# The third batch's second layer by eighths, and its expert mixing paired with the fourth's

## The chip, the cores and the metric

The kernel runs on one core of a Trainium2 chip, all of it in 32-bit floats. The metric is the device time of one execution in microseconds (us); the kernel before took 3224.32 us, the median of three runs (3222.8 to 3226.45).

The core has five instruction streams that run side by side and wait for each other through semaphores: TensorE (PE; its weight loads are shown as PEld) multiplies matrices, VectorE (DVE), ScalarE (ACT) and GpSimd (POOL) work on tiles, and SyncE (SP) issues nearly all of this kernel's DMAs, in program order. An instruction of SP that has to wait holds up every later DMA of that queue.

## The reference

Four batches of 2048 rows with 512 columns pass a windowed attention and then a feed-forward layer whose weights differ from batch to batch: a small gate, averaged over the batch, gives eight numbers, and the weights are the base weights plus eight expert weights scaled by them.

```python
# attention: 16 heads of 32, windows of 128 rows that see themselves and both neighbours, residual, layer norm
# then, for a batch with rows x1 (2048 x 512):
g  = mean over rows of (relu(x1 @ gw1.T + gb1) @ gw2.T + gb2)       # 8 numbers
W1b = W1 + sum_e g[e] * TW1[e]      # 2048 x 512      b1b likewise
W2b = W2 + sum_e g[e] * TW2[e]      # 512 x 2048      b2b likewise
out = x1 + layernorm(gelu(x1 @ W1b.T + b1b) @ W2b.T + b2b)
```

One mixed weight is 4 MB, and the experts of a layer are 32 MB, so each batch reads 64 MB of experts if it reads them for itself.

## The kernel before

**Attention first, then the feed-forward part.** The first 1674.4 us are attention, the gate and the layer norms. The rest is the feed-forward part in 16 blocks of 512 rows, `K` = 0 to 15; batch `b` is K // 4 and `k` = K % 4 the block in it. PE has its matmuls back to back; DVE, ACT, POOL and SP work beside it.

**The first layer of a block** is four *sets* (`c` = 0, 2, 4, 6), each a Winograd scheme of seven products in place of eight. A product is four matmuls 128x128x256 (L1023). `begin` (L1042) issues products A11 and S1 of a set; `middle` (L1065) issues A12, S2, S4, S3 and, after S2, calls `end` (L1086) of the set *before*, which issues that one's last product A22. Two sums on DVE lie in a set: `cpb` (L1080) after S4 and `cpv` (L1083) after S3; A22 adds into the bank of S3, so it can't start before `cpv` was read from there. Four places `step()` in `middle` let the mixing on DVE go on: before S2, before `cpb`, between `cpb` and `cpv`, and after `cpv`. The last set of a block (c = 6) has its `end` called by the second layer, after that one's first few matmuls.

**The second layer** has two forms. `second` (L1157) is seven products of 16 matmuls 128x256 (L1143; 112 in all), `end` of the last set coming after two of them. `second_deep` (L1237), used where the batch is in `DEEP`, applies the scheme twice, seven by seven products ("by eighths"), each four matmuls 128x128x128 (L1308; 196 in all). Of its outer products `o` = 0 to 6 each needs four differences of activations on DVE (`inner_sums`, L1233), held in two tiles of the `exps` pool. They are made during the outer product before, but those of o = 0 only when the last activations of c = 6 exist, and `end` of that set comes after the first four matmuls. POOL computes `t1`, `t2` (L1105, L1106, L1111) after each set and, at o = 2, a further difference into `t1` (L1344), the right side of o = 6. The layer norm's statistics of half of the rows come at o = 6 before the sum that follows `inner(4)`. DEEP is the fourth batch alone.

**Mixing.** The generator `mixer` (L106) goes through 64 chunks in a fixed order (batch, layer, eight chunks of two row groups), each with eight experts: one load of 512 KB (L123, three ahead, four buffers `exps`), one scalar_tensor_tensor (STT) `acc += g[e] * expert` on DVE (L155), and after the eighth four sums (L163 to L166) and the stores of the Winograd factors to DRAM (m1d, m2d, or m3d for DEEP). One `next(blend)` is one STT or the four sums: 9 steps to a chunk, 576 in all. 226 are placed in attention (MIXED, L961), the rest in the blocks: `mixing(1, 1, 1, 1)` in a set (2, 1, 1, 1 at c = 2; 0, 1, 0, 1 in block 0 and a batch's last block), and `mixing(3, 2, 3, 2, 2, 3, 2)` over the products of `second`.

**Inner sums of the deep weights.** `inner_mixer` (L174) has 14 steps for a deep batch: two loads of 256 KB from m3d into an `exps` buffer (two steps ahead), four sums on DVE (L205 to L208), three stores. Eight steps run in the second layer of block 11, six in the sets of block 12.

**Loads of the second layer's weights.** `load_second` (L1120) fetches 512 KB (`w2s`, six buffers; 14 loads in a plain block, 28 in a deep one) each time that a group of second-layer matmuls has been issued, so the six first loads of a block go out in the second layer of the block before. In a batch's last block `more_sums` (L1094) also loads the next batch's first-layer factors (5.5 MB, `load_first`).

Of the kernel before, what the change touches and what calls it, by code (L numbers as in the profile page):

```python
# [9 lines left out]
F32 = mybir.dt.float32  # L10
# [24 lines left out]
def sandwich(ctx: ExitStack, tc: tile.TileContext, x, w_qkv, gw1, gb1, gw2, gb2, w1, b1, w2, b2, tw1, tb1, tw2, tb2, out):  # L35
# [23 lines left out]
    gw1_sb = const.tile([P, KC, D], F32, name="gw1_sb")  # L59
# [20 lines left out]
    DEEP = (NB - 1,)  # L80
# [25 lines left out]
    def mixer():  # L106

        todo = [(b, s, c, e) for b in range(NB) for s in range(2) for c in range(HC) for e in range(NX)]
        ets, accs = {}, {}
# [5 lines left out]
        def load(n):  # L115
            b, s, c, e = todo[n]
            base, exps = ((w1, tw1), (w2, tw2))[s]
            if e == 0:
                acc = mix.tile([P, 2, D], F32, tag="acc", name=f"acc_{b}_{s}_{c}")
                nc.sync.dma_start(acc, halves(base)[c])  # L120
                accs[b, s, c] = acc
            et = mix.tile([P, 2, D], F32, tag="exps", bufs=4, name=f"exps_{b}_{s}_{c}_{e}")
            nc.sync.dma_start(et, halves(exps[e])[c])  # L123
            ets[n] = et
# [20 lines left out]
        for n in range(3):  # L145
            load(n)
        yield
        for n, (b, s, c, e) in enumerate(todo):
            if n + 3 < len(todo):
                load(n + 3)  # L150
            for f in late:
                f()
            late = []
            acc = accs[b, s, c]
            nc.vector.scalar_tensor_tensor(acc, ets.pop(n), g_all[b][:, e : e + 1], acc, ALU.mult, ALU.add)  # L155
            yield
            if e == NX - 1:
                del accs[b, s, c]
# [10 lines left out]
        for f in late:  # L169
            f()  # L170

    issued = {b: 0 for b in DEEP}

    def inner_mixer(b):  # L174

        todo = [(o, h) for o in order_deep for h in range(2)]
        loaded, late = {}, []

        def load(n):
            o, h = todo[n]  # L180
            two = slice(2 * h, 2 * h + 2)
            et = mix.tile([P, 4, 2, P], F32, tag="exps", bufs=4, name=f"inner_{b}_{o}_{h}")
            nc.sync.dma_start(et[:, :2], m3_d[b][:, o, 0:8:7, two, :])
            nc.sync.dma_start(et[:, 2:], m3_d[b][:, o, 3:7:3, two, :])
            loaded[n] = et

        def store(n, et):
# [7 lines left out]
        for n in range(2):  # L195
            load(n)
        yield
        for n in range(len(todo)):
            for f in late:
                f()  # L200
# [1404 lines left out]
```

## Time and profile before

| what | value |
|---|---|
| median of the runs (3) | 3224.32 us |
| the profiled execution: its time, its span | 3224.83 us, 3223.0 us |
| attention, gate, norms: until | 1674.4 us |
| PE busy | 3197.1 us (99%) |
| DVE, ACT, POOL busy | 2278.8 (71%), 1576.5 (49%), 676.5 us (21%) |
| granted TensorE clock | 0.998 |
| moved by DMA | 688.88 MB |
| expert loads `exps<-in_tw` | 512 of 512 KB |
| STTs (L155) | 512, 697.1 us, 1362 ns each |

The span runs from the first instruction to the last; the profiled execution's time is 1.8 us longer, and lies 0.5 us above the median. Busy shares are of the span. In the views of stretches each row begins with a stretch (us from the start of the span) and its length, then the busy time and count of instructions on each engine, the granted clock (PEclk), the mean busy share of the DMA engines and the rate. In a timeline a row gives start, duration, engine, line, operation, tile written from tiles read, the shape, and in brackets for how long the engine had been idle and what ended it. A view of waits gives the engine and the tile and line that wait, what they wait for, the sum in us, the count and the longest. A group of instructions has "busy, mean ns of one | idle time before, and what ended it".

### The profile page before, as it was taken

What the parts mean: (1) busy time and instruction counts of PE and PEld (TensorE: products, weight loads), DVE (VectorE), ACT (ScalarE), POOL (GpSimd) and SP (SyncE); (2) the same over time, 40 slices, a digit from 0 to 9 for tenths busy, and PEclk for the clock granted to TensorE, in tenths of its full rate; (3) what the DMA queues carried; (4) which work ended last, traced back from release to release, by engine and by line L of the source; (5) the groups of instructions that cost most, each with busy time, mean ns of one, the idle gap of its engine ahead of it and who ended that gap; (6) DMA issues with size and microseconds to landing.
All of it is one profiled execution on the core that took longest, in us unless ns stands there. A gap on an engine that the chain in (4) does not pass through costs nothing.

```text
span 3223.0 us, 61653 instructions
## 1 busy us (share of the span) xinstructions
PE 3197.1 (99%) x23862; PEld 2697.0 (84%) x23862; DVE 2278.8 (71%) x3307; ACT 1576.5 (49%) x4332; POOL 676.5 (21%) x847
## 2 busy tenths in 40 slices
PE   9999999999999999999999999999999999999998
PEld 7788888888788888878768888888888888889998
DVE  5766666888998889888865665677657667554555
ACT  3777777777777777777761222112222112222222
POOL 0111111111111111110112322323322323332233
PEclk9999999999999999999999999999999999999999
DMA  2111112455555556554677889999899999874555
GB/s 87 54 57 54 40 60 80 138 189 163 193 193 168 178 177 200 194 174 151 211 277 277 310 309 345 355 337 330 311 330 361 341 326 322 305 246 155 193 187 170
DMA packets 363334, 688.88 MB, mean 214 GB/s; under 512 B 27161, under 2 KB 115353, under 8 KB 357026
## 3 DMA queue, kind: packets, MB, share of 16 engines
q1 hardware_dynamic: 363042, 684.94, 61.4%
q8 instruction: 189, 3.10, 0.4%
q14 instruction: 103, 0.84, 0.1%
HBM read 567.39 MB, written 117.44 MB: 212 GB/s over the span
## 4 chain that ended last, share of the span: by engine, by line
PE 94%; DVE 2%; DMA 2%; ACT 1%; POOL 0%; issue 0%; SPq 0%; POOLq 0%; DVEq 0%; ACTq 0%
PE pm L518 23%; PE px L1023 13%; PE ptp L686 11%; PE px L1143 7%; PE sc L649 7%; PE pz L1023 6%; PE po L707 5%; PE pz L1143 5%; PE py L1023 3%; PE py L1143 3%; PE px L1308 2%; PE py2b L1143 2%; PE pz L1308 1%; PE pm L582 1%; PE ptx L340 1%; PE pto L311 1%
## 5 line engine op out<-in xcount | busy, mean ns | idle before, releaser
L155 DVE SCALAR_TENSOR_TENSOR acc<-exps,g,acc 128x1024 f32<-128x1024 f32 x512 | 697.1, 1362 | 66.1 <-DMA exps<-in_tw 60.1
L658 DVE TENSOR_REDUCE nm<-sc 128x2 f32<-128x768 f32 (+1 forms) x512 | 449.2, 918 | 206.8 <-PE sc L649 201.8
L671 ACT ACTIVATE pr<-sc,nm 128x384 f32<-128x384 f32 (+1 forms) x1024 | 572.8, 592 | 11.3 <-DVE nm L658 11.1
L691 ACT COPY prT<-ptp 128x512 f32<-128x512 f32 x732 | 382.9, 595 | 281.3 <-PE ptp L686 281.1
L686 PEld LDWEIGHTS ptp<-ident,pr 128*128 128x128 f32 x2944 | 318.0, 141 | 102.3 <-issue 89.8
L686 PE MATMUL ptp<-ident,pr 128*128 128x128 f32 x2944 | 378.7, 278 | 0.0
L1060 ACT COPY py<-px 128x512 f32<-128x512 f32 x63 | 36.0, 571 | 662.6 <-PE px L1023 662.4
L1023 PE MATMUL px<-tT,w 128*128 128x256 f32 x1512 | 350.1, 379 | 0.6 <-DVE cpv L1083 0.6
L1023 PEld LDWEIGHTS px<-tT,w 128*128 128x128 f32 x1512 | 286.9, 190 | 40.0 <-DVE cpv L1083 1.0
L649 PE MATMUL sc<-k,q 32*128 32x384 f32 (+2 forms) x2816 | 243.2, 423 | 3.7 <-ACT pr L671 3.5
L671 ACT ACTIVATION_READ_ACCUMULATOR pr<-sc,nm 128x1 f32 x1024 | 236.5, 231 | 0.0
L1080 DVE TENSOR_TENSOR cpb<-pz,cpb 128x512 f32<-128x512 f32 x63 | 43.4, 689 | 268.8 <-PE pz L1023 240.1
L96 POOL TENSOR_SCALAR ve_b<-mv_b 128x1 f32<-128x1 f32 x64 | 42.8, 669 | 819.2 <-DVE mv_b L94 819.2
L707 PEld LDWEIGHTS po<-prT,v 128*32 128x32 f32 x5888 | 152.2, 110 | 50.9 <-ACT pr L671 25.4
L707 PE MATMUL po<-prT,v 128*32 128x128 f32 x5888 | 189.7, 275 | 0.2
L649 PEld LDWEIGHTS sc<-k,q 32*128 32x128 f32 x2816 | 118.7, 184 | 74.4 <-issue 53.9
L1143 PE MATMUL px<-w2s,u 128*128 128x256 f32 x784 | 175.1, 379 | 0.0
L518 PE MATMUL pm<-xnT,wqkv 128*128 128x256 f32 x720 | 172.2, 382 | 0.0
L1105 POOL TENSOR_TENSOR t<-u 128x512 f32<-128x512 f32 x60 | 79.9, 1332 | 434.8 <-ACT u L1035 434.8
L1143 PEld LDWEIGHTS px<-w2s,u 128*128 128x128 f32 x784 | 149.0, 190 | 20.2
L518 PEld LDWEIGHTS pm<-xnT,wqkv 128*128 128x128 f32 x720 | 132.0, 190 | 16.7
L1074 ACT COPY cpb<-px 128x512 f32<-128x512 f32 x63 | 36.9, 585 | 182.0 <-PE px L1023 182.0
(295 smaller groups left out, 5911.6 us busy)
## 6 DMA issues: line engine op xcount, KB each, us to landing
exps<-in_tw SPq DMA_DIRECT2D x512, 512.0 KB, 6.0
w2s<-m2d SPq DMA_DIRECT2D x168, 512.0 KB, 8.1
w2s<-m3d SPq DMA_DIRECT2D x84, 512.0 KB, 4.7
acc<-in_w SPq DMA_DIRECT2D x64, 512.0 KB, 6.1
x<-in_x SPq DMA_DIRECT2D x64, 256.0 KB, 4.2
m1d<-acc SPq DMA_DIRECT2D x64, 256.0 KB, 6.3
w<-m1d SPq DMA_DIRECT2D x16, 1024.0 KB, 7.9
fxT<-xTd SPq DMA_DIRECT2D x16, 1024.0 KB, 8.5
```

Source lines behind the costliest of these rows:

```text
L155: nc.vector.scalar_tensor_tensor(acc, ets.pop(n), g_all[b][:, e : e + 1], acc, ALU.mult, ALU.add)
L518: nc.tensor.matmul(bank[u not in chain][:, half, :], lhsT=a[:, kc, ts(half, P)], rhs=b[:, kc, :], start=(u not in (2, 3, 4) and half == kc ...
L649: nc.tensor.matmul(scs[r // 2][:, r % 2, col : col + nj * W], lhsT=q[rows, g, ts(W_ % WB, W)], rhs=k_of[kb][rows, g, j0 * W : (j0 + nj) * ...
L658: nc.vector.tensor_reduce(st["nm"][:, h : h + 2], scs[u][:, :, : nk * W], AX.X, ALU.max, negate=True)
L671: nc.scalar.activation(pr[:, : nk * W], scs[r // 2][:, r % 2, : nk * W], AF.Exp, bias=st["nm"][:, h : h + 1], accum_out=st["den"][:, h : h ...
L686: nc.tensor.transpose(pt[:, r, :], st["pr"][g * 4 + r][:, ts(j, W)], ident)
L691: nc.scalar.copy(prT, pt)
L707: nc.tensor.matmul(po[r * E : (r + 1) * E, n, :], lhsT=v_of[kb][:, jj, h * E : (h + 1) * E], rhs=prT[:, r, :], start=(j == 0), stop=(j == ...
L1023: nc.tensor.matmul(bank[:, f, :], lhsT=factor[:, f, kc * P : (kc + 1) * P], rhs=right[:, kc, :], start=(start and f == 0 and kc == 0), sto ...
L1105: nc.gpsimd.tensor_tensor(t1s[c], b12, us[c][:, :, :Q], ALU.subtract)
L1143: nc.tensor.matmul(bank[:, t, :], lhsT=right(c - c % 2)[:, c % 2, ts(t, P)], rhs=w[:, c % (HC // 2), :], start=(start and c == 0 and t == ...
L1308: nc.tensor.matmul(bank, lhsT=right(p), rhs=w[:, p, :], start=(start and p == 0), stop=True, skip_group_check=True,)
```

## The change

- `DEEP` holds the third batch too, so blocks 8 to 11 use `second_deep`, and batch 2's second-layer weights are stored as m3d and get 14 inner steps.
- The mixer takes a list of steps. `mixing_plan` makes six. **Plan 0** (504 steps) has 40 chunks alone (both layers of batches 0 and 1, the first layer of batch 2) and, from the 28th of these on, after two of every three of them, one of eight *paired* chunks: the second-layer experts of batches 2 and 3, loaded once and used by two STTs. Batch 3's sums lie in the halves of the gate's weight tile, which becomes two tiles (`gw1_0`, `gw1_1`). This plan runs to the end of block 7's sets. **Plan 1**, in block 7's second layer (1, 2, 1, 1, 1, 1, 1) and block 8's sets: the 14 inner steps of batch 2, then 14 steps of batch 3's first layer. **Plans 2 to 4**, in the sets of blocks 9, 10, 11: 21 steps each; the last ends with five inner steps of batch 3. **Plan 5**, in block 12's sets: the other nine. The second layers of blocks 8 to 15 have no mixing step, `follow` passes from plan to plan.
- Counts: sets of blocks 8 to 15 have (0, 1, 1, 1) at c = 0 and (2, 1, 2, 1) else; those of blocks 0 to 7 (1, 1, 1, 1), or 2 for the first at c = 4, and at c = 2 too where the block isn't block 0 or a batch's last; `second` has 3 for each product.
- Stores that are due are issued before the next load, not after it; inner steps are loaded three ahead, not two.
- `load_second` fetches nothing of a block that isn't `wanted` yet: from block 1 on the first six loads of a block go out two per set, at its c = 2, 4 and 6.
- In `second_deep` POOL's difference for o = 6 moves from o = 2 (written to `t1`) to o = 4 (written to the upper half of `top`), and the statistics at o = 6 move behind the sum after `inner(4)`.

The diff, cut; `load_inner`, `sum_inner` and `store_inner` are the bodies of the old `inner_mixer`, and `halves` and `store` of the mixer are unchanged.

```diff
-    gw1_sb = const.tile([P, KC, D], F32, name="gw1_sb")
+    gw1_sb = [const.tile([P, 2, D], F32, tag=f"gw1_{j}", name=f"gw1_{j}") for j in range(2)]
...
-    DEEP = (NB - 1,)
+    DEEP = (NB - 2, NB - 1)
...
+    def mixing_plan():
+
+        todo = []
+
+        def chunk(batches, k, c, between=()):
+            waiting = [x for x in todo if x[0] == "later"]
+            for e in range(NX):
+                todo.append(("mix", batches, k, c, e))
+                if e == 1 and waiting:
+                    todo.remove(waiting[0])
+                    todo.append(("sum", *waiting[0][1:]))
+            todo.append(("sum", batches[0], k, c))
+            for b in batches[1:]:
+                todo.append(("later", b, k, c))
+            todo.extend(("inner", *x) for x in between)
+
+        LONE, pairs = 27, list(range(HC))
+        alone = [(b, k, c) for b, k in ((0, 0), (0, 1), (1, 0), (1, 1), (2, 0)) for c in range(HC)]
+        for n, (b, k, c) in enumerate(alone):
+            chunk((b,), k, c)
+            if (n - LONE) % 3 != 2 and n >= LONE and pairs:
+                chunk((2, 3), 1, pairs.pop(0))
+        plans = [[("sum" if x[0] == "later" else x[0], *x[1:]) for x in todo]]
+        todo.clear()
+        for c in range(HC):
+            chunk((3,), 0, c)
+        inner = {b: [("inner", b, o, h) for o in order_deep for h in range(2)] for b in DEEP}
+        plans.append(inner[2] + todo[:14])
+        plans.append(todo[14:35])
+        plans.append(todo[35:56])
+        plans.append(todo[56:] + inner[3][:5])
+        plans.append(inner[3][5:])
+        return plans
...
+    def mixer(todo):
+
+        loads = [x for x in todo if x[0] != "sum"]
+        ets = []
         late = []
...
+            if not loads:
+                return
+            kind, *what = loads.pop(0)
+            if kind == "inner":
+                ets.append(load_inner(*what))
+                return
+            batches, k, c, e = what
+            base, exps = ((w1, tw1), (w2, tw2))[k]
             if e == 0:
-                acc = mix.tile([P, 2, D], F32, tag="acc", name=f"acc_{b}_{s}_{c}")
-                nc.sync.dma_start(acc, halves(base)[c])
-                accs[b, s, c] = acc
-            et = mix.tile([P, 2, D], F32, tag="exps", bufs=4, name=f"exps_{b}_{s}_{c}_{e}")
+                for b in batches:
+                    if b < 3:
+                        acc = mix.tile([P, 2, D], F32, tag="acc", name=f"acc_{b}_{k}_{c}")
+                    else:
+                        assert gate_over
+                        acc = const.tile([P, 2, D], F32, tag=f"gw1_{c % 2}", name=f"acc_{b}_{k}_{c}")
+                    nc.sync.dma_start(acc, halves(base)[c])
+                    accs[b, k, c] = acc
+            et = mix.tile([P, 2, D], F32, tag="exps", bufs=4, name=f"exps_{batches[0]}_{k}_{c}_{e}")
             nc.sync.dma_start(et, halves(exps[e])[c])
-            ets[n] = et
+            ets.append(et)
...
+        for _ in range(3):
+            load()
+        yield
+        for kind, *what in todo:
+            if kind == "inner":
+                flush()
+                load()
+                et = ets.pop(0)
+                sum_inner(et)
+                late.append(lambda what=what, et=et: store_inner(*what, et))
+                yield
+            elif kind == "mix":
+                batches, s, c, e = what
+                flush()
+                load()
+                et = ets.pop(0)
+                for b in batches:
+                    flush()
+                    assert b in gated
+                    acc = accs[b, s, c]
+                    nc.vector.scalar_tensor_tensor(acc, et, g_all[b][:, e : e + 1], acc, ALU.mult, ALU.add)
+                    yield
+            else:
+                b, s, c = what
+                flush()
+                acc = accs.pop((b, s, c))
...
+        wanted = [0]
+
         def load_second():
 
-            if not coming:
+            if not coming or coming[0][0] > wanted[0]:
...
-                [t1],
+                [top[..., Q:]],
...
-                if o == 2:
+                if o == 4:
                     for p in range(PAIRS2):
-                        nc.gpsimd.tensor_tensor(t1[:, p], bottom[:, p, :, :Q], t2[p // 2][:, p % 2], ALU.subtract)
+                        t3 = top[:, p, :, Q:]
+                        nc.gpsimd.tensor_tensor(t3, bottom[:, p, :, :Q], t2[p // 2][:, p % 2], ALU.subtract)
...
+                inner(4, X, summed(2))
+                add(r[1, 1], X, r[1, 1])
+                run(dve, 1)
                 if o == 6:
...
-                inner(4, X, summed(2))
-                add(r[1, 1], X, r[1, 1])
-                run(dve, 1)
...
+        def follow():
+
+            nonlocal blend
+            assert next(blend, 0) == 0
+            plans.pop(0)
+            blend = mixer(plans[0])
+            next(blend)
...
+            if K > DEEP[0] * NBLK and len(plans) > 1:
+                follow()
             for c in range(0, HC, 2):
+                if K and c:
+                    wanted[0] = K
+                    for _ in range(2):
+                        load_second()
...
-                elif K == 0 or (k == NBLK - 1 and b + 1 < NB):
-                    step = mixing(0, 1, 0, 1)
+                elif K == 0 or (k == NBLK - 1 and b + 1 < DEEP[0]):
+                    step = mixing(*((2, 1, 1, 1) if c == 4 else (1, 1, 1, 1)))
                 else:
-                    step = mixing(*((2, 1, 1, 1) if c == 2 else (1, 1, 1, 1)))
-                if K // NBLK in DEEP and k == 0:
-                    step = lambda: next(inner, None)
+                    step = mixing(*((2, 1, 1, 1) if c in (2, 4) else (1, 1, 1, 1)))
+                if DEEP[0] * NBLK <= K:
+                    step = mixing(*((0, 1, 1, 1) if c == 0 else (2, 1, 2, 1)))
                 middle(n, S, before, step)
                 before = (n, S)
-                if b + 1 in DEEP and k == NBLK - 1 and c == HC - 2:
-                    assert next(blend, None) is None
-                    inner = inner_mixer(b + 1)
-                    next(inner)
...
             if b in DEEP:
+                assert next(blend, 0) == 0
                 products2 = second_deep(K, before, load_x1)
             else:
-                products2 = second(K, before, mixing(3, 2, 3, 2, 2, 3, 2), load_x1)
+                counts = (3, 3, 3, 3, 3, 3, 3)
+                if b + 1 == DEEP[0] and k == NBLK - 1:
+                    follow()
+                    counts = (1, 2, 1, 1, 1, 1, 1)
+                products2 = second(K, before, mixing(*counts), load_x1)
             for j, _ in enumerate(products2):
-                if b + 1 in DEEP and k == NBLK - 1:
-                    for _ in range((1, 2, 1, 1, 1, 1, 1)[j]):
-                        next(inner)
```

## The prediction

> **What bounds it.** I read the engines' busy shares first, then the stretches of the last eight blocks (cut where a block's first set begins), then the waits, then timelines.
>
> ```profile
> PE 3197.1 (99%) x23862; PEld 2697.0 (84%) x23862; DVE 2278.8 (71%) x3307; ACT 1576.5 (49%) x4332; POOL 676.5 (21%) x847
> ```
>
> PE never rests, so only fewer or cheaper matmuls gain, and any delay of PE is added to the end. The stretches are blocks 8, 11, 12, 13:
>
> ```profile
> 2448.46:2545.66 97.20, 96.96 (x449) 85.04 (x448) 69.98 (x84) 22.43 (x48) 32.62 (x30) 1.00 0.94 336
> ...
> 2739.48:2836.17 96.69, 96.69 (x449) 85.13 (x448) 47.32 (x74) 22.42 (x48) 27.10 (x32) 1.00 0.90 317
> 2836.17:2931.25 95.08, 93.07 (x617) 86.59 (x616) 61.24 (x125) 24.95 (x59) 30.28 (x29) 1.00 0.73 250
> 2931.25:3025.26 94.01, 92.81 (x618) 86.56 (x617) 45.95 (x96) 24.96 (x59) 28.14 (x29) 1.00 0.49 171
> ```
>
> A deep block lasts 94.01 us, a plain one 96.69, at a granted clock of 1.00. Blocks 8 to 10 run at a DMA share of 0.92 to 0.94 and 70 us of DVE, and still at PE's pace. Now the deep block's own losses, in PE's timeline of block 14:
>
> ```profile
> 3090.74 1.06 PE L1308 MATMUL pz<-w2s,u 128*128 128x128 f32 x8
> 3092.61 1.16 PE L1308 MATMUL px<-w2s,inner_right 128*128 128x128 f32 x8 [0.81 <-DVE y L1270]
> ```
>
> Groups of one inner product follow each other by 0.89 us; here it is 1.87, so 0.98 is lost, at o = 2. The DVE timeline shows why: a difference there takes 1.55 us (3090.80) against 0.68 when POOL is quiet, and POOL's L1344 runs from 3084.96 to 3091.81. At o = 6 (3118.27) another 0.55 goes where the statistics precede the sum that frees bank X. 94.01 − 0.98 − 0.55 = 92.5 us: the deep block without stalls.
>
> **Gain (a): blocks 8 to 11 become deep.** 97.20 + 96.70 + 97.12 + 96.69 = 387.7 against 4 × 92.5 = 370: **−17.7 us**. (By the matmuls: 112 at 0.432 us are 48.4, 196 at 0.223 are 43.8, 4.6 less a block.)
>
> **Gain (b): the POOL difference moves to o = 4, the statistics behind the sum.** −1.5 in each of blocks 12, 13, 14: **−4.5**; block 15 ends in statistics on DVE anyway, 0. From above: POOL's 6.85 us now fall on the differences of o = 4 and 5, four DVE operations of 0.68 us that can become 1.55, +3.5 against about 2 us that DVE idles there; stalls of up to 0.98 in each of eight blocks, +8, can't be excluded. I take 0, because no load or layer-norm work stands at o = 4.
>
> The Trainium skill ("SBUF — State Buffer", Who interferes with whom) says that VectorE and GpSimd share one pair of SBUF ports as an exclusive lock; the trace agrees in kind (0.68 against 1.55 to 1.76 us for operations with both inputs in SBUF; 0.69 for `cpv`, with one in PSUM), but by a full lock a difference under a POOL operation of 1.27 us would take up to 1.95, and the sum of (b)'s upper end would be near +12.
>
> **Cost (c): the last set before a deep second layer.** DVE in block 14, where the set has no mixing:
>
> ```profile
> 3070.43 0.69 DVE L1080 TENSOR_TENSOR cpb<-pz,cpb 128x512 f32<-128x512 f32 x1 [8.54 <-PE pz L1023]
> 3072.09 0.69 DVE L1083 TENSOR_TENSOR cpv<-px,cpv 128x512 f32<-128x512 f32 x1 [0.96 <-PE px L1023]
> 3072.70 0.68 DVE L1233 TENSOR_TENSOR inner_right<-u 128x512 f32<-128x512 f32 x1
> ...
> 3074.69 1.76 DVE L1233 TENSOR_TENSOR inner_right<-u,inner_right 128x512 f32<-128x512 f32 x1
> ```
>
> Product A22 adds into the bank that `cpv` reads. Within sets four products lie between (some 4.9 us of slack); here only the first inner product, 0.94 us, and A22 starts at 3072.83. The count (2, 1, 2, 1) puts two STTs between `cpb` and `cpv`: 3071.1 + 2 × 1.28 = 3073.7 in place of 3072.09, so A22 is 1.6 late, more where POOL works beside (three STTs took 5.72 us at 2311.14, 1.9 each). A third STT then stands before the four differences that product 1 of o = 0 and what follows needs: +1.3, of which A22 hides little. About **+3 us in each of blocks 9 and 10: +6** (2 to 8).
>
> **Cost (d): block 8's sets.** Plan 1 leaves six inner steps and 14 mixing steps there. Block 12 before shows what an inner step costs on SP and DVE:
>
> ```profile
> 2844.21 0.42 SPq L190 DMA_DIRECT2D m3d<-inner  x1
> 2844.72 0.38 SPq L191 DMA_DIRECT2D m3d<-inner  x1
> 2845.44 0.37 SPq L192 DMA_DIRECT2D m3d<-inner  x1
> 2846.66 0.37 SPq L183 DMA_DIRECT2D inner<-m3d  x1
> 2847.08 0.49 SPq L184 DMA_DIRECT2D inner<-m3d  x1
> ```
>
> ```profile
> 2844.67 0.43 DVE L205 TENSOR_TENSOR inner<-inner 128x256 f32<-128x256 f32 x1 [2.24 <-DMA inner<-m3d]
> ...
> 2848.09 0.43 DVE L205 TENSOR_TENSOR inner<-inner 128x256 f32<-128x256 f32 x1 [1.02 <-DMA inner<-m3d]
> ```
>
> 3.4 us a step, with loads two ahead. Three ahead with four buffers, the load goes into the buffer of the step just stored, so on SP stand three stores (1.4 us), their landing, two loads (0.9): with landings between 1.7 (the least in 2838 to 2862) and 4.1 (the median of these stores there) that is 4.0 to 6.4 us a step. SP is in order: behind it wait the mixing loads, `w2s` (two a set), first-layer loads and outputs; who waits for those is DVE, and through `cpb` and `cpv` PE. DVE's list for the sets: 6 × (4.0 to 6.4) = 24 to 38, 13 STTs of 1.36 = 18, four sums 2.7, eight additions of 0.69 = 5.5; 50 to 64 us. It begins 6 us into 48.4, so 42 are there: 8 to 22 late, at the end less some 5 that the last steps can lie behind: 3 to 22. I take **+14**, nearer the median landing.
>
> The skill ("DMA: Bandwidth & Descriptors", Two DMAs through the same engine are not ordered) has a dependent DMA wait for the first one's completion semaphore, so the store's landing can't be left out of the chain. Its fixed cost (Anatomy of one DMA, ~2.0 us, stated for the GpSimd path) would make, as an estimate, 2.3 us to a landing and 4.6 a step, and (d) +7.
>
> **Cost (e): block 11's sets.** Before, they moved 271 GB/s in 48.42 us (2739.48 to 2787.90), 13.1 MB. Added are seven expert loads (3.7 MB), five inner steps (5 MB), six `w2s` (3.1 MB): 25 MB, some 2 of them put off into the second layer. The second half of that block ran at 362 GB/s with the DMA share at 1.02, the best slice of the trace at 411: 23 MB take 56 to 64 us. **+10** (5 to 16): the inner stores also have to land before `second_deep`'s differences get their `exps` buffers.
>
> **Cost (f): block 12**, nine inner steps in the first two sets by the longer chain: four are loaded ahead, five cycles of 4.0 to 6.4 from 8 us on end at 28 to 40, and the place of the last can slip to 24 + 4.9: **+2** (0 to 11), near the low end because that block's DMA share was 0.73. **Cost (g): blocks 0 to 7** have 504 − 226 = 278 steps up to block 7's sets, where 224 stood; the pairs save 64 expert loads (512 to 448, 33.6 MB) and the 512 STTs stay. Three STTs to a product are 3.9 to 5.7 us in 6.9: **+1** (0 to 4). The `w2s` throttle I cost at nothing: two loads per set with 12 us until the next; without that cover, one load's landing (8.1 us less what precedes it) a block.
>
> Sum against the profiled execution: 3224.8 − 17.7 − 4.5 + 6 + 14 + 10 + 2 + 1 = 3235.6; that one lies 0.5 above the median of the runs, so **3235 us**.
>
> **Rivals.** *The waits stay short (other side).* Landings near 1.7 us and PE's slack taking most of it: (d) 3, (c) 4, (e) 5, the rest 0 make +12 against −22.2: 3214. For it: blocks 8 to 10 lose almost nothing now at a DMA share of 0.94. Against: the inner steps, which wait for a landing twice, are not among that work. The point that decides is whether the last `cpv` of block 8 comes within 10 us of S3's end (two thirds of (d)). *DMA saturation:* at 362 GB/s (e) is 16 and (d) 20, (c) 8: 3251. For it: the share of 1.02 in block 11's second half. *POOL's stall only moves:* (b) costs +1 in eight deep blocks in place of −4.5: 3247 with my other terms, 3226 with the short waits. *The change doesn't do what it says* is excluded by the rows of 96.69 and 94.01.
>
> **Chances.** My forecast 0.40, saturation 0.15, moved stall 0.12, short waits 0.33. A measurement tells 0.2%, 6.4 us, from no change: faster is under 3217.9, slower over 3230.8. Short waits fall about 0.28 under 3217.9 and the rest within; of the forecast 0.10 lies within and of the moved stall 0.03. Faster 0.28, same 0.18, slower 0.54. The range takes in short waits and most of saturation, 3208 to 3251; the forecast's own is 3224 to 3246.
>
> **What would show it.** Lengths of blocks 8 to 12: 106.5, 95.5, 95.5, 102.5, 94.5, and 92.5 for 13 and 14; PE waiting in blocks 8 and 11 for `cpb` or `cpv`, with DVE waiting for inner loads and SP for inner stores; PE waiting for `cpv` at c = 6 in 9 and 10; no wait of 0.8 at o = 2. It would be wrong if block 8 were under 97 us, if o = 4 stalled, or if a plain block lost over 1 us.

## The result

The changed kernel takes 3373.08 us (median of 4 runs, 3371.55 to 3376.27) against 3224.96 before: 1.0463 times as long, 95% interval 1.045 to 1.0476. The forecast was 3235 us, at most 3251. The sign was right, the size was not: +148 us in place of +11.

The page of the changed kernel, its first rows, the granted clock and the row of the mixing:

```profile
span 3372.1 us, 63491 instructions
...
PE 3219.5 (95%) x24534; PEld 2725.8 (81%) x24534; DVE 2422.1 (72%) x3620; ACT 1590.9 (47%) x4376; POOL 691.6 (21%) x851
...
PEclk9999999999999999999999999999997999899999
...
L240 DVE SCALAR_TENSOR_TENSOR acc<-exps,g,acc 128x1024 f32<-128x1024 f32 x512 | 690.2, 1358 | 136.2 <-DMA exps<-in_tw 131.9
```

The same row of the kernel before:

```profile
L155 DVE SCALAR_TENSOR_TENSOR acc<-exps,g,acc 128x1024 f32<-128x1024 f32 x512 | 697.1, 1362 | 66.1 <-DMA exps<-in_tw 60.1
```

PE now rests 5% of the span, the clock leaves nine tenths in two slices, and DVE waits twice as long for expert loads (131.9 us against 60.1) though there are 64 fewer of them. PE's two longest waits in sum over the whole span, then its wait for `cpv` before, then SP's longest wait that belongs to the inner steps (window from 1674 us), before and after:

```profile
PE px L1071 <- DVE cpv L1131: 101.6, 13, 26.0
PE py L1071 <- ACT py L1108: 11.9, 5, 5.8
```

```profile
PE px L1023 <- DVE cpv L1083: 0.6, 1, 0.6
```

```profile
SPq L183 <- DMA m3d<-inner: 3.6, 5, 0.9
```

```profile
SPq L111 <- DMA m3d<-inner: 67.1, 17, 7.8
```

`cpv` (L1131 now) is the wait that the prediction named, at 101.6 us. SP stands 67.1 us, 17 times, at the load of an inner step until the stores of an earlier one have landed. The stretches of blocks 7 to 12, cut as before:

```profile
2377.83:2493.24 115.41, 101.76 (x450) 87.97 (x449) 61.37 (x89) 22.91 (x48) 30.91 (x31) 0.94 0.86 297
2493.24:2637.24 144.00, 99.28 (x617) 90.68 (x616) 83.64 (x140) 25.73 (x59) 27.78 (x27) 0.83 0.74 246
2637.24:2742.88 105.64, 95.71 (x618) 88.16 (x617) 78.84 (x124) 25.21 (x59) 31.69 (x30) 0.95 0.80 275
2742.88:2852.08 109.20, 98.05 (x618) 89.81 (x617) 78.45 (x127) 25.44 (x59) 31.28 (x30) 0.94 0.78 272
2852.08:2976.17 124.09, 100.50 (x618) 91.98 (x617) 76.79 (x139) 25.40 (x59) 29.61 (x30) 0.88 0.88 311
2976.17:3079.73 103.56, 95.64 (x618) 88.21 (x617) 63.33 (x134) 25.20 (x59) 27.65 (x30) 0.97 0.72 243
```

Block 8 is the worst: 144.0 us at a mean clock of 0.83, and its DMA share (0.74) is lower than before (0.94), so the transfers don't fill the memory's time; they are issued late. The whole difference by blocks, before and after: blocks 1 to 6 together 583.1 and 611.1 (+28), block 7 96.7 and 115.4 (+18.7), 8 to 11 387.7 and 482.9 (+95.2), 12 95.1 and 103.6 (+8.5), 13 to 15 282.1 and 281.2. That is 149.5 us; attention ends 1.8 sooner, and what follows PE's last matmul is 1.4 longer.

By the starts of PE's matmuls in the feed-forward part, gaps above 0.7 us add up to 136 us of standing still (7 before); steps that are slower than 0.216 us, but shorter than such a gap, add up to 36 us (5 before), nearly all of it lower clock.

How block 8 loses 26 us in one place, its longest wait, DVE first, then SP, then PE:

```profile
2529.39 0.42 DVE L117 TENSOR_TENSOR inner<-inner 128x256 f32<-128x256 f32 x1 [3.06 <-DMA inner<-m3d]
...
2531.11 0.68 DVE L1128 TENSOR_TENSOR cpb<-pz,cpb 128x512 f32<-128x512 f32 x1
2541.45 1.28 DVE L240 SCALAR_TENSOR_TENSOR acc<-exps,g,acc 128x1024 f32<-128x1024 f32 x1 [9.65 <-DMA exps<-in_tw]
2546.83 1.29 DVE L240 SCALAR_TENSOR_TENSOR acc<-exps,g,acc 128x1024 f32<-128x1024 f32 x1 [4.10 <-DMA exps<-in_tw]
2548.03 0.68 DVE L1131 TENSOR_TENSOR cpv<-px,cpv 128x512 f32<-128x512 f32 x1
```

```profile
2520.76 0.37 SPq L111 DMA_DIRECT2D inner<-m3d  x1
...
2521.69 0.46 SPq L124 DMA_DIRECT2D m3d<-inner  x1
...
2522.72 0.39 SPq L126 DMA_DIRECT2D m3d<-inner  x1
2525.86 0.37 SPq L111 DMA_DIRECT2D inner<-m3d  x1
...
2529.71 2.29 SPq L190 DMA_DIRECT2D acc<-in_w  x1
2537.61 0.37 SPq L193 DMA_DIRECT2D exps<-in_tw  x1
2538.38 0.34 SPq L124 DMA_DIRECT2D m3d<-inner  x1
```

```profile
2548.77 3.78 PE L1071 MATMUL px<-tT,w 128*128 128x256 f32 x8 [26.02 <-DVE cpv L1131]
```

Stores at 2521.7 to 2523.1, the next load only at 2525.86, 5 us from step to step. The last inner step runs 38 us after the block began, and only then do the expert loads come, each behind the inner stores whose buffer it takes: 2537.61 the first that frees DVE. DVE waits 9.65 and 4.10 us for them with `cpv` behind it in its order. PE, which after S3 of this set has issued the four products of the next set that don't need `cpv`, stands from 2522.75 to 2548.77.

### The profile page after: what moved, and what is told of

It reads as the page before. It is cut to its first block, busy times and chain, and to the rows that moved or that the text cites. A ratio compares the mean times of both kernels' runs of the same rounds, so it can differ in the third digit from the quotient of the medians.

```text
span 3372.1 us, 63491 instructions
## 1 busy us (share of the span) xinstructions
PE 3219.5 (95%) x24534; PEld 2725.8 (81%) x24534; DVE 2422.1 (72%) x3620; ACT 1590.9 (47%) x4376; POOL 691.6 (21%) x851
## 4 chain that ended last, share of the span: by engine, by line
PE 81%; DMA 10%; DVE 5%; SPq 1%; issue 1%; ACT 1%; POOL 0%; DVEq 0%; POOLq 0%; ACTq 0%
PE pm L566 22%; PE ptp L734 10%; PE px L1071 10%; PE sc L697 6%; PE po L755 5%; PE pz L1071 5%; PE px L1358 5%; PE px L1193 4%; DMA exps<-in_tw 3%; PE pz L1193 2%; PE py L1071 2%; PE pz L1358 2%; DMA m3d<-inner 2%; DVE inner_right L1283 2%; PE py2b L1193 1%; PE py L1193 1%
## 5 line engine op out<-in xcount | busy, mean ns | idle before, releaser
L240 DVE SCALAR_TENSOR_TENSOR acc<-exps,g,acc 128x1024 f32<-128x1024 f32 x512 | 690.2, 1358 | 136.2 <-DMA exps<-in_tw 131.9
L739 ACT COPY prT<-ptp 128x512 f32<-128x512 f32 x732 | 382.9, 594 | 279.5 <-PE ptp L734 279.0
L1071 PE MATMUL px<-tT,w 128*128 128x256 f32 x1512 | 373.5, 397 | 101.6 <-DVE cpv L1131 101.6
L1071 PEld LDWEIGHTS px<-tT,w 128*128 128x128 f32 x1512 | 298.8, 199 | 149.8 <-DVE cpv L1131 106.6
L1358 PE MATMUL px<-w2s,inner_right 128*128 128x128 f32 x1344 | 180.8, 278 | 4.2 <-DVE y L1320 2.2
L1358 PEld LDWEIGHTS px<-w2s,inner_right 128*128 128x128 f32 x1344 | 164.9, 193 | 8.2 <-DVE y L1320 7.3
L1385 ACT COPY py<-px 128x128 f32<-128x128 f32 x56 | 14.0, 250 | 281.8 <-PE px L1358 141.5
```

What stands on the lines that cost most here:

```text
L240: nc.vector.scalar_tensor_tensor(acc, et, g_all[b][:, e : e + 1], acc, ALU.mult, ALU.add)
L739: nc.scalar.copy(prT, pt)
L1071: nc.tensor.matmul(bank[:, f, :], lhsT=factor[:, f, kc * P : (kc + 1) * P], rhs=right[:, kc, :], start=(start and f == 0 and kc == 0), sto ...
L1358: nc.tensor.matmul(bank, lhsT=right(p), rhs=w[:, p, :], start=(start and p == 0), stop=True, skip_group_check=True,)
```

## The experiments

Lengths of blocks in us, each from the first matmul of its first set to that of the next block, by the same view of stretches (block 15 to PE's last matmul; blocks 1 to 6, 9 and 10, 13 to 15 summed; the times are medians for the first two and the last, else single runs):

| kernel | time | 1-6 | 7 | 8 | 9+10 | 11 | 12 | 13-15 |
|---|---|---|---|---|---|---|---|---|
| before | 3225.0 | 583.1 | 96.7 | 97.2 | 193.8 | 96.7 | 95.1 | 282.1 |
| changed | 3373.1 | 611.1 | 115.4 | 144.0 | 214.8 | 124.1 | 103.6 | 281.2 |
| no throttle | 3342.7 | 598.5 | 112.6 | 144.8 | 204.8 | 117.7 | 103.0 | 281.5 |
| two ahead | 3340.3 | 607.1 | 105.3 | 122.9 | 214.5 | 125.1 | 103.8 | 279.3 |
| loads first | 3354.1 | 591.9 | 115.7 | 143.7 | 215.1 | 123.5 | 104.3 | 279.5 |
| the three | 3298.7 | 597.5 | 97.4 | 120.2 | 207.3 | 119.2 | 95.9 | 280.2 |
| one expert | 3297.5 | 611.0 | 115.6 | 118.9 | 186.0 | 104.7 | 102.6 | 280.2 |
| pairs, not deep | 3310.1 | 600.2 | 103.0 | 104.4 | 221.4 | 120.2 | 102.9 | 279.1 |
| last set free | 3370.8 | 613.3 | 117.0 | 135.1 | 211.7 | 123.1 | 109.5 | 280.3 |
| thinned | 3234.1 | 595.6 | 102.1 | 94.2 | 187.8 | 93.0 | 94.1 | 282.7 |
| last version | 3220.5 | 585.2 | 96.7 | 95.1 | 187.1 | 93.2 | 94.6 | 280.2 |

**No throttle.** The loads of the second layer's weights as before.

```diff
-            if not coming or coming[0][0] > wanted[0]:
+            if not coming:
...
-                if K and c:
-                    wanted[0] = K
-                    for _ in range(2):
-                        load_second()
```

> The changed kernel (3373 us) with the loads of the second layer's weights as in the kernel before: the first six of a block go out in the second layer of the block before. Theory throttle (two 512 KB loads at the second, third and fourth set put themselves ahead of the expert loads on SP and make the plain blocks 1 to 6 lose 28 us): blocks 1 to 6 return to about 97 to 98 us each, total 3330 to 3345. Theory inner chain (stores, their landing and the loads into the same buffer, in order on SP, set the pace): blocks 7 to 12 keep their 19 + 51 + 13 + 17 + 32 + 9 us and the total moves less than 30. Theory store order: blocks 1 to 6 keep their losses too, total 3365 to 3375.

Measured 3342.7, 30 us less. Blocks 2, 3 and 6 are back at 96.7, 96.7 and 97.2, but 1, 4 and 5 take 105.1, 100.7 and 102.1 (99.8, 105.4 and 100.3 with the throttle). In sum blocks 1 to 6 gain 12.6 of the 28 us, and blocks 9 to 11 another 16.4. The inner chain is untouched (SP's wait 75.5 us, block 8 at 144.8).

**Two ahead.** An inner step is loaded two steps ahead, into a buffer stored a step earlier.

```diff
-            if not loads:
+            if not loads or (loads[0][0] == "inner" and len(ets) > 2):
                 return
...
                 flush()
                 load()
+                if loads and loads[0][0] == "mix" and len(ets) < 4:
+                    load()
                 et = ets.pop(0)
                 sum_inner(et)
```

> The changed kernel with the inner steps loaded two ahead, as in the kernel before, in place of three (the load goes into a buffer whose stores were issued a step earlier). Theory inner chain: the wait of SP for m3d<-inner (67 us, 17 times) falls under 20, block 7 returns to 97 to 102 us, block 8 from 144 to 105 to 120, block 12 from 103.6 to 95; total 3300 to 3330. Rival, crowded queue (each step's DMAs are issued behind waits for DVE, whatever the depth of the prefetch): SP's wait goes over to other items, blocks 7 and 8 lose as much, total 3355 to 3380.

```profile
SPq L111 <- DMA m3d<-inner: 5.1, 8, 0.9
```

That is SP's wait in this run (67.1 before): the chain through the stores' landing is gone. Block 7 gains 10 us and block 8 21, the total 33: 3340.3, over the expected 3330, and block 12 gains nothing. The mechanism holds in 7 and 8, though both stay above the lengths expected (105.3 and 122.9); in 11 and 12 something else holds PE up.

**Loads first.** The next expert load is issued ahead of the stores that are due.

```diff
-                flush()
                 load()
+                flush()
                 et = ets.pop(0)
                 for b in batches:
```

> The changed kernel with the next expert load issued ahead of the stores that are due, as in the kernel before (for mixing steps; inner steps as they are). Theory store order (a load stands behind three to six stores that wait for the sums on DVE): blocks 1 to 6 lose under 10 us in place of 28, and blocks 9 and 10 gain some 3 each; total 3335 to 3355. Rivals throttle and density (three steps to a product): nothing moves by more than 10 us, total 3363 to 3380.

3354.1, 19 us less, all of it in blocks 1 to 6 (19.2), and none in 9 and 10. What blocks 1 to 6 still lose, 8.8 us, is what the theory left them; for blocks 9 and 10 it was wrong.

**The sums moved alone**, in the kernel before.

```diff
-                [t1],
+                [top[..., Q:]],
...
-                if o == 2:
+                if o == 4:
...
+                inner(4, X, summed(2))
+                add(r[1, 1], X, r[1, 1])
+                run(dve, 1)
                 if o == 6:
...
-                inner(4, X, summed(2))
-                add(r[1, 1], X, r[1, 1])
-                run(dve, 1)
```

> The kernel before with POOL's difference moved from o = 2 to o = 4 and the statistics at o = 6 behind the sum, and nothing else of the change. The prediction: blocks 12 to 14 lose 1.5 us each, the stall of 0.8 at o = 2 and that of 0.4 at o = 6 are gone, total 4.5 us under the kernel before (ratio 0.9986). Rival, the stall moves to o = 4: the waits of TensorE for y of 5.7 us stay within 1.5 us, total within 2 us of before (ratio 0.9995 to 1.001).

```profile
PE px L1308 <- DVE y L1270: 1.5, 5, 0.8
```

The wait of 5.7 us falls to 1.5 (window from 2800 us), so the stall went and did not move to o = 4; blocks 12 to 15 together are 3.4 us shorter. The ratio, 0.9995 with an interval of 0.9986 to 1.0005, can't tell it from no change.

**The three at once.**

> The changed kernel with all three at once: no throttle on the second layer's weights, inner steps two ahead, the next expert load ahead of the stores. Alone they took 30, 33 and 19 us off 3373. Theory separate places (the throttle and the store order act in blocks 1 to 6 and 9 to 10, the prefetch depth in 7 and 8): they add up, 3285 to 3300. Rival, one queue (all three only shorten the same line of waiting items on SP, and the next item takes the place): 3305 to 3330. Under either, blocks 8 and 11 stay above 110 us.

3298.7, 74 us less, where the three alone add up to 82, inside the first theory's range. By blocks they are not separate, so the near match is in part luck: blocks 1 to 6 gain 13.6 us where the single runs add up to 36, and blocks 7, 8 and 12 gain 50 where they add up to 33. What is left in blocks 1 to 6, 14 us, has no wait for `cpv` behind it any more; PE's waits there (window 1674 to 2400 us; they end at 1786, 2083 and 2184) are for `py`, a copy made by ScalarE, but for one of 0.7 us:

```profile
PE py L1073 <- ACT py L1110: 10.3, 3, 4.0
```

Block 7 is at 97.4. Blocks 8 to 11 still lose 75 us against four of 93.0.

**One expert.**

```diff
-            chunk((3,), 0, c)
+            todo.extend([("mix", (3,), 0, c, 0), ("sum", 3, 0, c)])
```

> The changed kernel without experts 2 to 8 of batch 3's first layer (only the first is loaded and added; the four sums and the stores stay): 56 loads of 512 KB and 56 STTs less in blocks 8 to 11; the output is not the reference's. Theory mixing behind inner steps (in 8 and 11 the expert loads stand behind stores that wait to land, in 9 and 10 the STTs of the last set hold up cpv): blocks 9 and 10 fall from 105.6 and 109.2 to 93 to 95, block 8 from 144 to 108 to 118, block 11 from 124 to 98 to 108; total 3280 to 3305. Rival, the second layer by eighths itself (its difference tiles take the buffers, its sums crowd DVE): blocks 9 and 10 stay above 100, total over 3320.

The kernel leaves out seven of the eight experts of batch 3's first layer. It takes 3297.5 us. The stretch of block 9 (block 10's has the same length, and PE is as busy):

```profile
2611.05:2704.06 93.01, 92.81 (x619) 86.56 (x617) 52.15 (x107) 24.98 (x59) 27.94 (x30) 1.00 0.62 216
```

This is the second layer by eighths without mixing: 93.01 us, PE busy 92.81, against 96.69 plain. So the gain is there, 15.7 us if four blocks take 93.0, and the 29 us that blocks 9 and 10 lose is all mixing. Block 8, with its inner steps, still takes 118.9.

**Pairs, not deep.** `DEEP` is the fourth batch alone again (its uses in the step counts written as numbers); the second layers of blocks 7 to 11 do no mixing.

```diff
-    DEEP = (NB - 2, NB - 1)
+    DEEP = (NB - 1,)
...
-        plans.append(inner[2] + todo[:14])
+        plans.append(todo[:14])
...
-                counts = (3, 3, 3, 3, 3, 3, 3)
-                if b + 1 == DEEP[0] and k == NBLK - 1:
+                counts = (3, 3, 3, 3, 3, 3, 3) if K < 7 else 7 * (0,)
+                if K == 7:
                     follow()
-                    counts = (1, 2, 1, 1, 1, 1, 1)
```

> The changed kernel with the third batch's second layer plain (no inner steps for it; blocks 7 to 11 do no mixing in their second layers; all the rest, the pairs and the mixing of batch 3's first layer in the sets of blocks 8 to 11 included, as changed). Theory inner steps and eighths (they cost the most in blocks 7 to 10): block 7 returns to 97 to 99, block 8 to 97 to 105, 9 and 10 to 97 to 102; total 3265 to 3290. Rival, the mixing's place (21 steps crowded into the sets): blocks 9 and 10 stay at 105 to 110 and block 8 above 110; total over 3310.

3310.1: both were half right. Blocks 7 and 8 fall by 12 and 40 us, the price of the inner steps with what stands behind them. But blocks 9 and 10, plain now, take 109.5 and 112.0: 21 mixing steps in four sets stall PE whatever follows the sets.

**Last set free.**

```diff
-                    step = mixing(*((0, 1, 1, 1) if c == 0 else (2, 1, 2, 1)))
+                    step = mixing(*{0: (0, 1, 1, 2), 2: (2, 2, 2, 1), 4: (3, 2, 2, 1), 6: (2, 0, 0, 0)}[c])
```

> The changed kernel with the steps of the sets in blocks 8 to 12 counted otherwise: (0, 1, 1, 2) at c = 0, (2, 2, 2, 1) at c = 2, (3, 2, 2, 1) at c = 4 and (2, 0, 0, 0) at c = 6, 21 as before; none now stands between the two sums of the last set or between them and the differences of the second layer. Theory short slack at the set's end (prediction's cost (c)): the stalls at c = 6, 9.2 us in block 9 and 8.0 in block 10, fall under 2 and these blocks to 97 to 100. Rival, late loads (DVE waits for expert loads wherever the STT stands): the stalls move to c = 2 and c = 4 and blocks 9 and 10 stay within 4 us of 105.6 and 109.2.

3370.8. The waits of the last set go, and others come one set earlier, at the A22 of c = 4 (10.9 us to 2685.35 in block 9, 6.6 to 2788.54 in block 10); the blocks are 106.1 and 105.6 in place of 105.6 and 109.2, as the rival had it. The prediction's reason for cost (c) falls: the place in the set wasn't the cause.

**Thinned.** The three undone, and the steps spread: MIXED raised to 279 steps in attention, batch 3's first layer appended to plan 0 behind the pairs (first 487 entries before block 7's second layer, then none in block 8, 12 and 13 entries in 9 and 10), at most four steps in a set.

```diff
-        MIXED = (1, 0, 1, 1, 2, 1, 1, 2, 2, 1, 1, 1, 2, 1, 2, 2)
+        MIXED = (1, 1, 2, 1, 2, 1, 2, 2, 2, 1, 1, 2, 2, 2, 2, 2)
...
-            if (n - LONE) % 3 != 2 and n >= LONE and pairs:
+            if n >= LONE and pairs:
                 chunk((2, 3), 1, pairs.pop(0))
...
+        plans = [todo[:487]]
         inner = {b: [("inner", b, o, h) for o in order_deep for h in range(2)] for b in DEEP}
-        plans.append(inner[2] + todo[:14])
-        plans.append(todo[14:35])
-        plans.append(todo[35:56])
-        plans.append(todo[56:] + inner[3][:5])
-        plans.append(inner[3][5:])
+        plans.append(inner[2])
+        plans.append(todo[487:499])
+        plans.append(todo[499:])
+        plans.append(inner[3][:6])
+        plans.append(inner[3][6:])
...
-                    step = mixing(*((0, 1, 1, 1) if c == 0 else (2, 1, 2, 1)))
+                    step = mixing(*((0, 1, 1, 1) if c == 0 else (2, 1, 0, 0) if c == 6 else (1, 1, 1, 1)))
```

> As the run with all three undone, but with the work spread out: 279 mixing steps in attention in place of 226, the paired chunks after the 34th lone one, batch 3's first layer as far as it goes in blocks 0 to 7 (four steps in the fourth product and two in the last, not three and three), block 8's sets with the six inner steps alone, 13 and 14 mixing steps in the sets of blocks 9 and 10, batch 3's inner steps six in block 11 and eight in block 12; at most four steps in a set, and none after cpb in the last set. Theory density (a set of 12.1 us holds about four steps; six, with slowed STTs and the output sums, are 13 to 15 us of DVE): blocks 8 to 11 take 93 to 96 us each, total 3205 to 3225 if attention takes the 53 steps at no cost. Rival, the eighths' difference tiles in the pool of the expert loads delay each block's first loads however few they are: blocks 9 and 10 stay above 99, total over 3230. If attention is full, it ends later than 1675 us by up to 53 x 1.36 = 72 us.

3234.1, 9 us over the theory's range. Blocks 8 to 11 take 94.2, 94.5, 93.3 and 93.0: the density theory holds there, though the run doesn't tell fewer STTs on DVE from fewer loads on SP. Attention ends 2.9 us later. What is left lies in the plain blocks, a wait that was in the changed kernel too (`py` after ScalarE, 11.9 us there, 9.6 here). ScalarE's and GpSimd's rows in block 3:

```profile
1987.38 1.52 ACT L1467 ACTIVATE y<-y,shift,rs_d 128x512 f32<-128x512 f32 x2 [6.85 <-POOL shift L1466]
1988.81 0.57 ACT L1112 COPY py<-px 128x512 f32<-128x512 f32 x1
```

```profile
1986.02 1.57 POOL L1466 TENSOR_SCALAR shift<-mv_d,rs_d 128x1 f32<-128x1 f32 x2
```

The layer norm's scaling stands ahead of the copy that PE waits for, and waits itself for statistics that DVE makes behind the STTs of the last product, and for what GpSimd makes of them: beside the STTs two of its steps take 1.15 and 1.46 us, where the same two just before took 0.22 and 0.57.

**The last product light**, twice: 14 steps fewer in the plain second layers and nine of them behind block 8's inner steps, or seven fewer and six there.

```diff
-                counts = (3, 4, 3, 3, 3, 3, 2)
+                counts = (3, 3, 3, 3, 3, 3, 1)
...
-        plans.append(inner[2])
+        plans.append(inner[2] + todo[473:482])
```

> As the run with the work thinned out (3234), with (3, 3, 3, 3, 3, 3, 1) steps in the second layer of blocks 1 to 6 and the 14 steps that this leaves over in the sets of blocks 8 to 10 (nine mixing steps behind the six inner ones in block 8, 15 each in 9 and 10). Theory late statistics (in blocks 1, 3 and 7 STTs ahead of the statistics make ScalarE's scaling, and behind it its copies, late; PE waits 3 to 4 us for py): these three waits go, blocks 1, 3, 4 and 7 fall from 103.9, 103.2, 98.4, 102.1 to 97 to 99, total 3212 to 3224 (ratio 0.996 to 1.000). Rival: nine steps behind the inner ones stall block 8 again (over 100) and eat the gain: 3225 to 3245.

> The same with (3, 3, 3, 4, 3, 3, 1), so that seven steps fewer are left over (six in block 8, 13 each in 9 and 10). By the theory of late statistics 3210 to 3222, block 8 under 96; by density in the fourth product, where POOL's four sums slow the STTs to 1.7 to 1.9 us, blocks 1 to 6 lose 1 to 2 us each: 3220 to 3230.

3241.4 (1.0050, 1.0035 to 1.0065) and 3227.9 (1.0008, 0.9999 to 1.0018). Blocks 1 to 6 gain 4.7 and 9.3 us in sum (590.9 and 586.3), so the last product's steps did hold up the copies; block 0 loses 1.5 and 4.3, and block 8 loses 12 and 6 again: the more mixing behind its inner steps, the longer it is.

**Six inner steps alone** in block 8 (plan 0 to entry 486 and (3, 3, 3, 4, 3, 3, 1) in the second layers, block 0's fourth product 3), then the same with 290 and with 300 steps in attention; the last version's lines:

```diff
-        LONE, pairs = 33, list(range(HC))
+        LONE, pairs = 36, list(range(HC))
...
-        MIXED = (1, 1, 2, 1, 2, 1, 2, 2, 2, 1, 1, 2, 2, 2, 2, 2)
+        MIXED = (1, 1, 2, 2, 2, 2, 2, 2, 2, 1, 1, 2, 2, 2, 2, 2)
...
-                counts = (3, 3, 3, 4 if K else 3, 3, 3, 1)
+                counts = (3, 3, 3, 3, 3, 3, 1)
```

> As the run before (3227.9), with six more expert steps in the sets of blocks 4 to 7 so that block 8 has the six inner steps alone and blocks 9 and 10 have 13 mixing steps each, and three steps, not four, in the fourth product of block 0. Theory: the wait of 4.8 us for cpv at the end of block 8's sets goes (100.4 to about 94), the wait of 2 us for the gate's sums in block 0 goes; 3216 to 3222, ratio 0.9975 to 0.9995. Rival: the six steps put ScalarE's copies late again in blocks 4 to 7, 2 us each: 3224 to 3230, no faster than before.

> As the run before (3227.9), with 290 mixing steps in attention, so that block 7's sets have some seven in place of eighteen; the paired chunks begin after the 36th lone one. Theory density in block 7 (18 mixing steps beside the loads of the next batch's first-layer weights, 7 MB on the same queue, make cpv late three times): block 7 falls from 109.8 to 97 to 99, blocks 8 to 15 stay at 93 to 94, attention ends within 1 us of 1677.8; total 3214 to 3220 (ratio 0.997 to 0.9985). Rival, the queue alone (loads of the next weights in front of w2s and of the first inner loads, with few mixing steps too): block 7 stays above 104, total 3222 to 3230.

> The same with 300 steps in attention and three, not four, in the fourth product of every block, so that block 7's sets have almost none. Theory: attention has room for ten more at under 1 us, every plain block under 98: 3212 to 3218. Rival, attention is full (the 53 added so far cost 3 us): it ends later by up to 10 x 1.36 = 14 us, 3220 to 3232.

3227.9 (1.0010, 1.0001 to 1.0019): block 8 is 94.1, and block 7, which took the steps, 109.8. With 290 in attention 3227.7 (1.0009, 1.0000 to 1.0018), block 7 102.5, between the two theories; its wait was now that of ScalarE behind late statistics (3.8 us). With 300 and three steps to every product but the last **3220.5 us, 0.9986 of the time before (0.9977 to 0.9996)**: the only version of the changed kernel that is faster than the kernel before, by some 4.5 us. It is 2.5 above what the theory allowed and inside the range of the rival, by which attention is full; the four times before it, from the lighter last product on, lie in their rivals' ranges too. Its stretch of block 8:

```profile
2459.04:2554.13 95.09, 93.48 (x618) 86.78 (x616) 61.19 (x123) 24.96 (x59) 26.94 (x27) 1.00 0.70 240
```

The feed-forward part is 12.8 us shorter than before (1526.2 against 1539.0); attention with 74 more steps ends 8.6 us later (1682.96 against 1674.4), which is 0.12 us a step for STTs of 1.36. That price is rough: with the same 279 steps attention ended between 1677.3 and 1679.9 in four runs.

## Why the prediction was right and wrong

**Right.** (a) 92.5 us for a deep block without stalls: 93.0 measured, a gain of 15.7 in place of 17.7 (12.3 in the last version, whose blocks 8 to 11 take 375.4). (b) the two moves in the deep second layer: 3.4 us of trace in place of 4.5, no stall at o = 4, though the time of that run alone can't be told from no change. The new wait for `cpv`, with DVE waiting for loads and SP for inner stores, was the right mechanism, and the worst block was the one named.

**(d), block 8: 14 predicted, 51 measured (144.0 − 93.0).** The inner chain itself was inside its bounds: five steps took 5 to 8 us each and the last ran 38 us after the block began, where 6 + (24 to 38) was said. The term that failed is "13 STTs of 1.36 = 18 us". Fourteen steps took from 2531 to 2589, 58 us. I counted DVE's work and took its loads as made in time, having written myself that they stand on SP behind the chain. With the prefetch back at two the block falls to 122.9; without most of the mixing to 118.9; without inner steps to 104.4.

**(c), blocks 9 and 10: 6 predicted, 29 measured.** The step that failed is the reason, "the last set before a deep second layer": with those places freed the waits only moved, and with a plain second layer they stayed. The sets are too dense. Before, a set had four or five steps and DVE's output sums of the block before; (2, 1, 2, 1) are six. DVE ahead of the wait of 9.1 us that ends in block 9 at 2695.17:

```profile
2683.26 5.81 DVE L240 SCALAR_TENSOR_TENSOR acc<-exps,g,acc 128x1024 f32<-128x1024 f32 x3
2688.99 0.68 DVE L1128 TENSOR_TENSOR cpb<-pz,cpb 128x512 f32<-128x512 f32 x1
2691.89 2.63 DVE L240 SCALAR_TENSOR_TENSOR acc<-exps,g,acc 128x1024 f32<-128x1024 f32 x2 [2.22 <-DMA exps<-in_tw]
2694.43 0.68 DVE L1131 TENSOR_TENSOR cpv<-px,cpv 128x512 f32<-128x512 f32 x1
```

Three STTs beside GpSimd's sums take 5.81 us, and the next wait 2.22 us for a load. How much is DVE's own work and how much late loads stays open.

**(e), block 11: 10 predicted, 31 measured**, of which 19 are the mixing (104.7 with one expert). The bound of 23 MB at the memory's rate wasn't the limit: the block ran at 311 GB/s, its first 78 us at 291 with a DMA share of 0.83. Without the throttle it is 6.4 shorter, and with the three undone, six inner steps and no mixing in its sets (thinned) it takes 93.0; the rest was not split further.

**(g), blocks 0 to 7: 1 predicted, 47 measured.** Four things were priced too low or not at all. "The `w2s` throttle I cost at nothing": 30 us by its run, 12.6 of it in blocks 1 to 6. The stores before the loads, described but without a price: 19 us. Three STTs to a product, the +1: with the other two undone blocks 1 to 6 still lose 14 us, and PE's waits there are nearly all for late copies; in the thinned kernel they lose 12.5, and nine of these go with one step in the last product in place of two. These shares overlap and can't be added. And block 7's second layer, where eight inner steps run, has no term in my sum at all: the loads of its own weights stand on SP behind inner loads that wait for stores. SP's rows, and PE's wait, which the loads of 2467.83 end:

```profile
2453.87 0.37 SPq L126 DMA_DIRECT2D m3d<-inner  x1
2461.74 0.37 SPq L111 DMA_DIRECT2D inner<-m3d  x1
...
2467.31 0.46 SPq L112 DMA_DIRECT2D inner<-m3d  x1
2467.83 0.93 SPq L1183 DMA_DIRECT2D w2s<-m2d  x2
...
2469.76 0.77 SPq L126 DMA_DIRECT2D m3d<-inner  x1
2477.98 0.37 SPq L111 DMA_DIRECT2D inner<-m3d  x1
```

```profile
2475.45 2.90 PE L1193 MATMUL px<-w2s,u 128*128 128x256 f32 x6 [8.43 <-DMA w2s<-m2d]
```

From the last store's issue to the next load 7.9 and 8.2 us, where I had 1.7 and 4.1 as the ends for a landing. With the inner steps two ahead this wait of PE is gone.

**(f), block 12: 2 predicted, 8.5 measured**, inside the range of 0 to 11; no single edit cured it, all three undone did (95.9).

**Not in the sum: the clock.** Some 31 of the 149 us are lower clock after PE's waits. The stretches before and after the wait that ended at 2548.77 (columns as above, the clock third from the end):

```profile
2520.00:2523.00 3.00, 2.75 (x13) 2.09 (x11) 1.19 (x3) 0.21 (x1) 0.00 (x0) 1.00 0.35 97
2549.00:2553.00 4.00, 4.00 (x10) 3.19 (x11) 2.38 (x2) 1.07 (x4) 3.20 (x2) 0.50 1.02 372
2553.00:2557.00 4.00, 4.00 (x19) 3.53 (x19) 3.90 (x4) 1.16 (x4) 0.27 (x1) 0.99 0.86 287
```

For four us the clock is 0.50, so the wait costs 2 us more than its length. The Trainium skill ("TensorE: Matmul & The Clock Gate", What's actually happening) says that a free-running window of some 3.4 us of idleness brings the array to half rate until about one busy window has passed. The trace agrees with the half rate and with a recovery of 3 to 6 us; gaps shorter than that window brought it too, as the last section shows.

The rivals: none of them held. "DMA saturation" had the right sign and the wrong resource (its terms add up to 3249, not the 3251 written, and the best slice that I had read was 420 GB/s, not 411). The "short waits" needed landings near 1.7 us where the stores of the inner steps took 3.3 (2504.97 to 2508.24) to 8.2; by their deciding point they fell only just, since the last `cpv` of block 8 began some 12 us after S3, at 2588.95. The stall at o = 2 did not move: 1.5 us of its wait were left with the sums moved alone.

## What to carry to other kernels

Work that feeds an engine through one in-order queue is priced by that queue: write down, for each moved load, everything that is issued ahead of it and what that waits for, and add the consumers' durations only after. A load into a buffer that was stored just before waits for the store's landing; one step less of prefetch took that wait from 67 to 5 us. The gain of the cheaper matmuls was real all along, and came out when the sets held at most four or five mixing steps and the rest stood in attention, where a step cost 0.12 us on average.

## What the runs showed of the hardware beyond that

The lower clock is no fixed price. What follows is taken over the feed-forward parts of all runs, with PE's gaps measured from the start of one matmul to the next, which is 0.4 us more than the wait in the views. After gaps of 1.2 to 2.2 us the granted clock did not fall. Gaps of 2.25 (pairs not deep, 1915.9) and 2.63 us (changed kernel, 2787.6) lost 1.8 us more, while one of 3.61 (changed, 2193.0) and one of 3.39 (last version, 2023.3) lost 0.1. Those above 4 us in the first layer's matmuls lost 1.4 to 3.2 us more, hardly depending on the length: the gap of 26.4 us lost 2.2, no more than those of 5. Of the 38 gaps of 2.2 to 4.0 us, 20 lost at most 0.1 us more, one 0.5, and 17 lost 1.5 to 3.1. So a wait of 2 to 4 us may cost 1.5 to 3 us more, or nothing, and its length doesn't tell which.
